# One attention stream and one mixing stream over all eight sequences, and the norm's power by logarithm and exponential

## The chip, the core and the metric

The kernel runs on one core of a Trainium2 chip, in one launch. The core has five engines with queues of their own: TensorE (PE in the profile; PEld is its weight load), VectorE (DVE), ScalarE (ACT), GpSimd (POOL) and SyncE (SP, which here only issues DMAs). The metric is the device time of one execution in microseconds; the time given is the median of the executions shown.

## What is computed

The reference is two transformer layers over 8 sequences of 256 tokens with 256 channels, all in float32:

```python
x = x + attention(layernorm(x))      # w = x W^T; q, k, v are w, RMS-normed per head (16 heads of 16)
                                     # score = softmax over j + softmax over i; y = (score v) W
x = x + experts_0(layernorm(x))      # 4 experts, 2 per token: silu(x w1) * (x w3) @ w2, weighted
                                     # by the router, plus a shared expert on every token
x = x + time_mixing(layernorm(x))    # RWKV: k, v, r of shifted tokens; a recurrence over time;
                                     # layer norm; times sigmoid(r); output matrix
x = x + experts_1(layernorm(x))      # 8 experts, 2 per token, gated, with biases
```

The RMS norm needs, for each token and head, (mean of 16 squares + eps) to the power -1/2.

## The kernel before, in words

Tokens stay in SBUF as eight tiles `xs[b]` of 128 partitions by 2 by 256. The sequences are split in two groups, 0 to 4 and 5 to 7 (`GROUPS`), and each expert layer has one object per group: `one` and `two` in layer 0, `three` and `four` in layer 1 (class `Experts`).

**Experts.** For each sequence `norm` (layer norm on DVE with a small power on POOL), `flip` (transpose on PE, copy on ACT) and `judge` (router matmuls) fill the group's logits. `choose` turns them into slots by some forty small DVE operations and two matmuls, so that every expert's tokens lie together, in tiles of 128 rows. `sends` writes each token's normed row to its two slots in DRAM, by indirect DMAs that POOL issues (20 for the large group, 12 for the small). `tiles` is a software pipeline over the tiles (23 and 15 in layer 0, 27 and 19 in layer 1): fetch the rows, transpose, up-projection, activation, transpose, down-projection, a copy `yg` out of PSUM (L839), and a write to DRAM (L840). `combine` gathers each token's two results by indirect DMAs on POOL and adds them to `xs` on DVE (L868); the gathers wait until all tiles of the group are written. `shared` is the shared expert of layer 0, or the bias term of layer 1.

**Attention** (`attention_bounded`). `steps` lays the parts of each sequence out over numbered steps, four steps from one sequence to the next: `norm`, `project_in` (L436, then the RMS norm in L441 to L447), two steps later `turn` (transposes of the normed n, L456), then scores and exponentials (L480, L485, L493), `values` (L511), `to_tokens`, `turn_back`, `project_heads` (L551, L554), and after that the group's `norm`, `flip`, `judge`. PE's order in this stage is the order of the program (`manual_schedule`); the other engines' orders, and PE's elsewhere, come from a planner that goes by the program's order as priority and by modelled times. Each engine then works through its queue in that fixed order.

**Mixing** (`time_mixing`). `rwkv(b)` yields eight times; a sequence starts when the one before has done four of its steps, so two are in flight. Two multiplications (L949, L952) and the small powers of its norms are on POOL, most of the rest on DVE.

**Order.** `weave` interleaves streams in proportion to the numbers given. Before the change the program runs: attention of group 0; `one.choose`; sends and shared of `one` with the first six steps of group 1's attention; 12 tiles of `one` with the rest of that attention; `two.choose`; sends of `two` with the other tiles of `one`; combine of `one`, shared of `two`; mixing of group 0 with the tiles of `two`; `three.choose`; combine of `two`; the weights of layer 1; sends and shared of `three` with six steps of group 1's mixing; tiles of `three` with the rest of it; `four.choose`; sends and shared of `four` with the last tiles of `three`; combine of `three` with the tiles of `four`; combine of `four`, after which the outputs leave.

Of the kernel before, what the change touches and what calls it, by code (L numbers as in the profile page):

```python
# [9 lines left out]
F32 = mybir.dt.float32  # L10
# [57 lines left out]
def two_layers(  # L68
# [57 lines left out]
    minus_half = filled("minus_half", -0.5, (P, TT * NH))  # L126
# [9 lines left out]
    awt = load(const, attn_wt, [P, NC, D], "(c p) o -> p c o", nc.scalar, p=P, name="awt")  # L136
    gv = const.tile([P, 3, DH], F32, tag="gv", name="gv")
    nc.scalar.dma_start(out=gv, in_=g123.partition_broadcast(P))
    aw = load(const, attn_w, [P, NC, D], "(c p) o -> p c o", nc.scalar, p=P, name="aw")
# [265 lines left out]
    def attention_bounded(ap1, ap2, ep, fresh):  # L405
# [21 lines left out]
        def norm(b):  # L427
            seq[b] = dict(xT=turned(layer_norm(ap2, b, "xn"), ap2, "xnT", fresh()[0], nc.scalar))

        def project_in(b):  # L430
# [10 lines left out]
            nc.scalar.activation(sq, pw4, AF.Square)  # L441
            rr = ap2.tile([P, TT, NH], F32, tag="rr", name="rr")
            nc.vector.tensor_reduce(rr, sq, AX.X, ALU.add)
            nc.vector.tensor_scalar(rr, rr, 1.0 / DH, RMS_EPS, ALU.mult, ALU.add)  # L444
            nc.gpsimd.tensor_tensor(rr, rr, minus_half.rearrange("p (t h) -> p t h", h=NH), ALU.pow)  # L445
# [76 lines left out]
        def to_tokens(b, u):  # L522

            q = seq[b]
            if u == 0:
                q["y"] = ap2.tile([P, TT, NH, DH], F32, tag="y", name="y")
# [15 lines left out]
        def turn_back(b):  # L542
            y = seq[b]["y"].rearrange("p t h d -> p t (h d)")
            seq[b]["yT2"] = turned(y, ap2, "yT2", fresh()[0], nc.scalar)
# [11 lines left out]
        def steps(seqs, after):  # L556
# [11 lines left out]
            for i, b in enumerate(seqs):  # L568
# [12 lines left out]
                for k, f in enumerate(after):  # L581
                    at(n + 7 + k, f, b)
            order = (norm, turn, exponentials, project_in, to_tokens, values, turn_back, project_heads) + tuple(after)
            for n in range(max(late) + 1):
                for f, args in sorted(late.get(n, []), key=lambda x: order.index(x[0])):
                    f(*args)
                yield
# [24 lines left out]
    class Experts:  # L612
# [7 lines left out]
        def __init__(self, layer, k, weights, lnp, mp, rt, ps, mm):  # L620
# [7 lines left out]
            self.last = self.seqs == GROUPS[-1]  # L628

        def norm(self, b):  # L630
            if not self.xns:
                self.logit = self.rt.tile([P, self.nt, self.n_experts], F32, tag="logit", name="logit", bufs=2)
            self.xns[b] = layer_norm(self.lnp, b, "xm", bufs=max(len(g) for g in GROUPS))
# [19 lines left out]
        def choose(self):  # L653
# [22 lines left out]
            self.route()  # L676

# [111 lines left out]
        def tiles(self):  # L789
# [46 lines left out]
            def down(j):  # L836
                py = times(hTs.pop(j), self.weights[1], experts.pop(j), n_hidden, D)
                yg = mp.tile([P, D], F32, tag="yg", name="yg", bufs=3)
                nc.vector.tensor_copy(yg, py)  # L839
# [36 lines left out]
    def time_mixing(rp, rp1, wkv_w, ps, pk):  # L876
# [20 lines left out]
        def rwkv(b):  # L897
# [36 lines left out]
            ex, e1 = new("ex", 3), new("e1")  # L934
# [124 lines left out]
    def layers(is_bounded):  # L1059
# [4 lines left out]
        with ExitStack() as pctx, ExitStack() as ctx0, ExitStack() as actx:  # L1064
# [14 lines left out]
            one, two = (Experts(0, k, w0, lnp, mp, rt, ps, mm) for k in range(2))  # L1079
            with ExitStack() as p1:  # L1080
                psum.update(pool=p1.enter_context(tc.tile_pool(name="p1", bufs=1, space=PSUM)), ps=4, sc=4)
                if is_bounded:
# [3 lines left out]
                    steps = attention_bounded(ap1, ap2, ep, lambda: (ps, sc))  # L1086
                    with tc.manual_schedule(engines={ENG.PE}):
                        for _ in steps(GROUPS[0], (one.norm, one.flip, one.judge)):
                            pass
                else:  # L1090
                    for b in GROUPS[0]:
                        one.norm(b), one.flip(b), one.judge(b)
            with ExitStack() as p2:
                psum.update(pool=p2.enter_context(tc.tile_pool(name="p2", bufs=1, space=PSUM)), mm=2, ps=3, sc=3)
                one.choose()
                tiles = one.tiles()
                if is_bounded:
                    attention = steps(GROUPS[1], (two.norm, two.flip, two.judge))
                    with tc.manual_schedule(engines={ENG.PE}):
                        weave((one.sends(), 10), (take(attention, 6), 6), (one.shared(), 5))  # L1100
                        weave((take(tiles, 12), 12), (attention, 13))
                    actx.close()
                else:
                    weave((one.sends(), 10), (one.shared(), 5))
                    weave((take(tiles, 12), 12))
                    for b in GROUPS[1]:
                        two.norm(b), two.flip(b), two.judge(b)
# [3 lines left out]
            two.choose()  # L1111
            weave((two.sends(), 6), (tiles, 13))
# [7 lines left out]
            mixing = time_mixing(rp, rw, wkv_w, ps, sc)  # L1120
            three, four = (Experts(1, k, None, lnp, None, rt, ps, mm) for k in range(2))

            def norm_of(experts):
                def f(b):
                    experts.norm(b), experts.flip(b), experts.judge(b)

                return f

            tiles = two.tiles()
            weave((one.combine(), 5), (two.shared(), 3), (take(tiles, 2), 2))  # L1130
            weave((mixing(GROUPS[0], norm_of(three)), 36), (tiles, 15))
            three.choose()
            weave((two.combine(), 3))
# [7 lines left out]
            ahead = mixing(GROUPS[1], norm_of(four))  # L1141
            weave((three.sends(), 10), (three.shared(), 5), (take(ahead, 6), 6))
            tiles = three.tiles()
            weave((take(tiles, 17), 17), (ahead, 16))
            four.choose()
            weave((take(tiles, 3), 3))
            weave((four.sends(), 6), (four.shared(), 3), (tiles, 9))
# [83 lines left out]
```

## Time and profile before

| | us |
|---|---|
| median of three executions (979.26 to 980.01) | 979.57 |
| the profiled execution | 982.58 |
| its span, first to last instruction | 980.8 |
| PE busy / PEld busy | 748.6 / 460.7 |
| DVE busy | 501.1 |
| ACT busy | 356.0 |
| POOL busy | 261.7 |

The span is the time from the first to the last profiled instruction. Busy time is an engine's own working time; what an engine idles is not by itself lost, since another may set the end. The granted clock tells how much of TensorE's full rate it was given. A row of the timeline gives start and duration in microseconds, engine, line, operation, what is written and read, and in brackets how long the engine had idled and what released it.

### The profile page before, as it was taken

How to read it: one execution, taken by the hardware profiler on the slowest of the kernel's cores; microseconds unless marked ns; L12 is line 12 of the kernel's file. 1: busy time of each engine (PE TensorE's matmuls, PEld its weight loads, DVE VectorE, ACT ScalarE, POOL GpSimd, SP SyncE). 2: the span in 40 equal slices, each digit the busy share in tenths (PEclk: the TensorE clock that was granted, in tenths of full speed). 3: DMA queues.
4: the chain of work that ended last, by engine and by line, in shares of the span. 5: the costliest groups of instructions: out<-in, count | busy, mean ns of one | idle time of the engine just before them, and what ended most of it. 6: DMA issues, size and time to landing. Idle time of an engine off the chain costs nothing. (4 is left out here: it accounts for less than half of the span.)

```text
span 980.8 us, 11031 instructions
## 1 busy us (share of the span) xinstructions
PE 748.6 (76%) x3248; PEld 460.7 (47%) x3248; DVE 501.1 (51%) x1208; ACT 356.0 (36%) x693; POOL 261.7 (27%) x338
## 2 busy tenths in 40 slices
PE   2588885668899997998798869923777876897890
PEld 1234444553445464666565646612444544453450
DVE  4476774224234324113578567766557684335442
ACT  1376651135566722221154345300225252232230
POOL 4423201830200001304412112052723131516104
PEclk9998895897889997999799779965678798799995
DMA  8910000210000002212210000015811111315313
GB/s 275 315 58 1 1 1 6 80 44 11 16 17 22 28 27 76 97 44 89 62 33 17 27 12 11 17 53 168 289 59 44 43 38 33 108 65 165 115 61 105
DMA packets 57762, 66.97 MB, mean 68 GB/s; under 512 B 7480, under 2 KB 51552, under 8 KB 57696
## 3 DMA queue, kind: packets, MB, share of 16 engines
q1 hardware_dynamic: 50016, 48.79, 15.4%
q0 software_dynamic: 6144, 16.79, 5.4%
q10 hardware_dynamic: 1536, 0.60, 0.2%
q8 instruction: 31, 0.51, 0.2%
q14 instruction: 35, 0.29, 0.1%
HBM read 38.61 MB, written 27.54 MB: 67 GB/s over the span
## 5 line engine op out<-in xcount | busy, mean ns | idle before, releaser
L812 PE MATMUL mm<-v1s,xgT 128*128 x184 | 97.8, 654 | 0.8 <-ACT xgT L806 0.7
L865 POOL DMA_INDIRECT y<-back,slot x64 | 62.1, 970 | 126.4 <-DMA back<-yg 94.0
L806 ACT COPY hT<-ps 128x256 f32<-128x256 f32 (+1 forms) x84 | 39.3, 467 | 131.5 <-PE ps L804 131.5
L736 POOL DMA_INDIRECT sent<-xm,slot x64 | 63.8, 997 | 71.7 <-DVE pick L711 53.9
L812 PE MATMUL mm<-w1s,xgT 128*128 x152 | 78.9, 642 | 1.1 <-issue 0.3
L812 PE MATMUL mm<-w3s,xgT 128*128 x152 | 73.1, 603 | 3.3 <-DVE h L834 3.3
L480 PE MATMUL sc<-qT,kT 32*128 32x512 f32 x256 | 62.9, 741 | 15.0 <-ACT e L493 13.1
L177 POOL TENSOR_TENSOR rs<-mv,eps_ln 128x2 f32<-128x2 f32 x32 | 7.6, 238 | 248.8 <-DVE mv L175 226.8
L494 DVE TENSOR_REDUCE s<-e 128x2 f32<-128x512 f32 x96 | 60.2, 678 | 25.6 <-ACT e L493 25.3
L493 ACT ACTIVATE e<-sc,minus 128x512 f32<-128x512 f32 x96 | 59.2, 694 | 37.1 <-PE sc L480 37.1
L812 PE MATMUL mm<-w2s,hT 128*128 x304 | 72.5, 380 | 0.0
L834 DVE TENSOR_TENSOR h<-h,mm 128x512 f32<-128x512 f32 x38 | 25.9, 681 | 76.5 <-PE mm L812 65.8
L445 POOL TENSOR_TENSOR rr<-rr,minus_half 128x32 f32<-128x32 f32 x8 | 43.5, 5437 | 76.2 <-DVE rr L444 76.2
L804 PEld LDWEIGHTS ps<-ident,h 128*128 128x128 f32 x244 | 31.7, 147 | 66.8 <-issue 34.1
L804 PE MATMUL ps<-ident,h 128*128 128x128 f32 x244 | 44.1, 289 | 23.0 <-DVE h L828 11.1
L839 DVE COPY yg<-mm 128x256 f32<-128x256 f32 x84 | 35.3, 420 | 50.3 <-PE mm L812 50.1
L825 DVE TENSOR_TENSOR hb<-mm,b1rows 128x512 f32<-128x512 f32 x46 | 31.6, 688 | 53.2 <-PE mm L812 47.8
L806 ACT COPY xgT<-ps 128x256 f32<-128x256 f32 x84 | 30.9, 370 | 74.1 <-PE ps L804 73.6
L812 PEld LDWEIGHTS mm<-w2s,hT 128*128 128x128 f32 x304 | 54.8, 190 | 5.9
L812 PE MATMUL mm<-v2s,hT 128*128 x184 | 49.2, 390 | 1.4 <-ACT hT L806 0.8
L868 DVE SCALAR_TENSOR_TENSOR x<-y,share,x 128x256 f32<-128x256 f32 x64 | 30.7, 484 | 38.1 <-DMA y<-back,slot 38.0
L812 PEld LDWEIGHTS mm<-w3s,xgT 128*128 128x128 f32 x152 | 29.2, 195 | 42.4 <-issue 34.2
(208 smaller groups left out, 1396.0 us busy)
## 6 DMA issues: line engine op xcount, KB each, us to landing
xg<-sent SPq DMA_DIRECT2D x84, 128.0 KB, 2.0
back<-yg SPq DMA_DIRECT2D x84, 128.0 KB, 1.7
sent<-zero SPq DMA_DIRECT2D x46, 128.0 KB, 1.9
x<-in_x_dram SPq DMA_DIRECT2D x8, 256.0 KB, 3.9
w1s<-in_w_dram SPq DMA_DIRECT2D x4, 512.0 KB, 9.6
w3s<-in_w_dram SPq DMA_DIRECT2D x4, 512.0 KB, 9.2
w2s<-in_w_dram SPq DMA_DIRECT2D x4, 512.0 KB, 10.4
v1s<-in_v1g_dram SPq DMA_DIRECT2D x8, 256.0 KB, 5.9
```

The lines of the kernel that those rows point to most:

```text
L445: nc.gpsimd.tensor_tensor(rr, rr, minus_half.rearrange("p (t h) -> p t h", h=NH), ALU.pow)
L480: nc.tensor.matmul(pa, lhsT=q["kT"][rows, u, ts(t, P)], rhs=q["qT"][rows, u], start=True, stop=True)
L493: nc.scalar.activation(e, pa, AF.Exp, bias=minus)
L494: nc.vector.tensor_reduce(q["s"][:, t, h : h + 2], e, AX.X, ALU.add)
L736: inst = nc.gpsimd.indirect_dma_start(out=self.sent, out_offset=self.index(k, t), in_=self.xns[self.seqs[t // TT]][:, t % TT, :], in_offse ...
L804: nc.tensor.transpose(pt[:, c, :], src[:, ts(c, P)], ident)
L806: nc.scalar.copy(to, pt)
L812: nc.tensor.matmul(po.unsqueeze(1), lhsT=lhsT[:, c, :], rhs=w[:, ds(e, 1), c, :], start=(c == 0), stop=(c == n - 1))
L825: nc.vector.tensor_tensor(hb.unsqueeze(1), ph.unsqueeze(1), self.weights[2][:, ds(e_dve, 1), :], ALU.add)
L839: nc.vector.tensor_copy(yg, py)
L865: nc.gpsimd.indirect_dma_start(out=y, out_offset=None, in_=self.back, in_offset=self.index(k, at))
L868: nc.vector.scalar_tensor_tensor(xs[b][:, t, :], y, self.share[:, k, at : at + 1], xs[b][:, t, :], ALU.mult, ALU.add)
```

## The change

- The power of the RMS norm leaves POOL. The mean of squares plus eps stays in `ms`; ACT takes its logarithm and the exponential of -1/2 of that, and three DVE operations make one Newton step on the result.
- Attention is one stream over all eight sequences. The choice of `one` is a step of that stream, as soon as its last sequence is judged; from there its sends and shared experts are woven into the stream, with `ps` as their PSUM banks. The choice of `two` is a step of the stream as well. All tiles of `one` follow it, with sends and shared of `two`.
- Mixing is one stream over all eight sequences, cut into pieces: 18 steps with the tiles of `two`, three with its combine, then the weights of layer 1, steps until `three` is chosen, 12 with sends and shared of `three`, the rest with 8 of its tiles. The norms and routers of `three` and `four`, and their choices, are called as sequences end (`take_in`).
- `xm` has eight buffers instead of five; `xn`, `xnT`, `y`, `yT2` and `ex` have one instead of two.
- In layer 0 the copy `yg` is ACT's instead of DVE's. The load of `gv` is issued before that of `awt`.

```diff
@@ project_in
+            ms = ap2.tile([P, TT, NH], F32, tag="ms", name="ms")
+            nc.vector.tensor_reduce(ms, sq, AX.X, ALU.add)
+            nc.vector.tensor_scalar(ms, ms, 1.0 / DH, RMS_EPS, ALU.mult, ALU.add)
             rr = ap2.tile([P, TT, NH], F32, tag="rr", name="rr")
-            nc.vector.tensor_reduce(rr, sq, AX.X, ALU.add)
-            nc.vector.tensor_scalar(rr, rr, 1.0 / DH, RMS_EPS, ALU.mult, ALU.add)
-            nc.gpsimd.tensor_tensor(rr, rr, minus_half.rearrange("p (t h) -> p t h", h=NH), ALU.pow)
+            nc.scalar.activation(rr, ms, AF.Ln)
+            nc.scalar.activation(rr, rr, AF.Exp, scale=-0.5)
+            r3 = ap2.tile([P, TT, NH], F32, tag="r3", name="r3")
+            nc.vector.tensor_tensor(r3, rr, rr, ALU.mult)
+            nc.vector.scalar_tensor_tensor(r3, r3, -0.5, ms, ALU.mult, ALU.mult)
+            nc.vector.scalar_tensor_tensor(rr, r3, 1.5, rr, ALU.add, ALU.mult)
@@ steps
-                for k, f in enumerate(after):
-                    at(n + 7 + k, f, b)
+                m = after[b]
+                at(n + 7, m.norm, b)
+                at(n + 8, m.flip, b)
+                at(n + 9, m.judge, b)
+                if b == m.seqs[-1]:
+                    at(n + 9, m.choose)
@@ Experts
+        def take_in(self, b):
+            self.norm(b), self.flip(b), self.judge(b)
+            if b == self.seqs[-1]:
+                self.choose()
...
-            self.xns[b] = layer_norm(self.lnp, b, "xm", bufs=max(len(g) for g in GROUPS))
+            self.xns[b] = layer_norm(self.lnp, b, "xm", bufs=B)
...
-                nc.vector.tensor_copy(yg, py)
+                if self.layer:
+                    nc.vector.tensor_copy(yg, py)
+                else:
+                    nc.scalar.copy(yg, py)
@@ rwkv
-            ex, e1 = new("ex", 3), new("e1")
+            ex, e1 = new("ex", 3, bufs=1), new("e1")
@@ layers, bounded path
+                    one.mm = ps
                     with tc.manual_schedule(engines={ENG.PE}):
-                        for _ in steps(GROUPS[0], (one.norm, one.flip, one.judge)):
-                            pass
...
-                psum.update(pool=p2..., mm=2, ps=3, sc=3)
-                one.choose()
...
-                    attention = steps(GROUPS[1], (two.norm, two.flip, two.judge))
-                        weave((one.sends(), 10), (take(attention, 6), 6), (one.shared(), 5))
-                        weave((take(tiles, 12), 12), (attention, 13))
+                        attention = steps(range(B), group_of)
+                        while not one.chosen:
+                            next(attention)
+                        weave((one.sends(), 10), (attention, 12), (one.shared(), 5))
+                    one.mm = mm
...
-            two.choose()
-            weave((two.sends(), 6), (tiles, 13))
+            weave((two.sends(), 6), (one.tiles(), 25), (two.shared(), 3))
...
-            weave((one.combine(), 5), (two.shared(), 3), (take(tiles, 2), 2))
-            weave((mixing(GROUPS[0], norm_of(three)), 36), (tiles, 15))
-            three.choose()
-            weave((two.combine(), 3))
+            weave((one.combine(), 5), (take(tiles, 2), 2))
+            weave((take(mixing, 18), 18), (tiles, 15))
+            weave((take(mixing, 3), 3), (two.combine(), 3))
...
-            ahead = mixing(GROUPS[1], norm_of(four))
-            weave((three.sends(), 10), (three.shared(), 5), (take(ahead, 6), 6))
+            while not three.chosen:
+                next(mixing)
+            weave((three.sends(), 10), (three.shared(), 5), (take(mixing, 12), 12))
             tiles = three.tiles()
-            weave((take(tiles, 17), 17), (ahead, 16))
-            four.choose()
-            weave((take(tiles, 3), 3))
-            weave((four.sends(), 6), (four.shared(), 3), (tiles, 9))
+            weave((take(tiles, 8), 8), (mixing, 12))
+            weave((four.sends(), 6), (four.shared(), 3), (tiles, 21))
             weave((three.combine(), 5), (four.tiles(), 21))
```

## The prediction

> **What bounds the kernel now.** I read the page first: TensorE is busy 76% of the span, at a clock granted below full.
>
> ```profile
> span 980.8 us, 11031 instructions
> PE 748.6 (76%) x3248; PEld 460.7 (47%) x3248; DVE 501.1 (51%) x1208; ACT 356.0 (36%) x693; POOL 261.7 (27%) x338
> PE   2588885668899997998798869923777876897890
> PEclk9998895897889997999799779965678798799995
> ```
>
> So PE sets the time where it is full, and holes and slow clock are what can be won. Then the table of stretches, cut where the stages change (columns: stretch, length and busy us of PE, PEld, DVE, ACT, POOL, clock, DMA):
>
> ```profile
> 28.00:160.00 132.00, 101.59 (x708) 54.72 (x708) 82.74 (x211) 71.84 (x173) 32.51 (x30) 0.88 0.18 60
> 160.00:228.00 68.00, 45.95 (x188) 33.80 (x188) 22.66 (x69) 17.20 (x30) 31.92 (x26) 0.81 0.14 47
> 228.00:371.00 143.00, 130.56 (x603) 69.62 (x602) 49.31 (x114) 79.38 (x140) 7.95 (x7) 0.89 0.07 22
> 371.00:452.00 81.00, 76.69 (x290) 49.34 (x290) 21.56 (x82) 21.48 (x39) 12.51 (x14) 0.94 0.22 70
> 484.00:669.00 185.00, 144.49 (x572) 98.42 (x570) 132.74 (x276) 70.84 (x106) 41.10 (x48) 0.88 0.08 26
> 669.00:716.00 47.00, 23.68 (x80) 15.87 (x81) 25.17 (x80) 8.02 (x16) 25.35 (x26) 0.57 0.73 242
> ```
>
> In order: attention of sequences 0-4; choice, sends and shared experts; attention of 5-7 with 12 tiles; 11 tiles; mixing of 0-4; the hole between the mixing groups. Two stretches are poor: 160 to 228, and 669 to 716, where PE works half the time at 0.57 clock. Third, the timeline inside one attention period (start, duration):
>
> ```profile
> 82.87 0.68 DVE L443 TENSOR_REDUCE rr<-sq 128x32 f32<-128x512 f32 x1
> 83.58 0.18 DVE L444 TENSOR_SCALAR rr<-rr 128x32 f32<-128x32 f32 x1
> 83.84 5.43 POOL L445 TENSOR_TENSOR rr<-rr,minus_half 128x32 f32<-128x32 f32 x1 [3.48 <-DVE rr L444]
> 89.30 0.69 DVE L447 TENSOR_TENSOR n<-ps,rr 128x512 f32<-128x512 f32 x1 [5.54 <-POOL rr L445]
> ```
>
> PE has nothing from 85.6 to 90.05 (4.42 us before L456): POOL's power is late, once a period of 23.2 us. Last, the mixing rhythm, from DVE's timeline:
>
> ```profile
> 588.18 0.69 DVE L895 TENSOR_TENSOR dx<-x 128x512 f32<-128x512 f32 x1 [2.68 <-ACT x L900]
> 625.72 0.67 DVE L895 TENSOR_TENSOR dx<-x 128x512 f32<-128x512 f32 x1
> 638.47 0.69 DVE L895 TENSOR_TENSOR x<-x,sc 128x512 f32<-128x512 f32 x1 [1.75 <-PE sc L993]
> 668.84 0.69 DVE L895 TENSOR_TENSOR x<-x,sc 128x512 f32<-128x512 f32 x1 [0.68 <-PE sc L993]
> ```
>
> A sequence begins (dx) 37 us after the one before and ends (x) 50 us after its own begin, 43 us when alone: latency of a chain, two in flight.
>
> **What the Trainium skill says.** "ScalarE: Activation LUTs", Table sets: Ln and Exp lie together in one set, natural_log_exp_and_others; What ACT_TABLE_LOAD costs: 1283 ns and a drain of some 1380. The trace has 1283 ns, and the next activation 11 ns later where its input was there, so I take 1.28 and no drain. "TensorE: Matmul & The Clock Gate", Part 1: after about 3.4 us idle PE runs at half rate for as long. It agrees: clock 0.92 over 66.8 to 85.6, but 1.00 over 70 to 85.6, just after a hole of 4.3 us. "GPSIMD Engine Reference", section 3, has elementwise work about twice as slow as on VectorE; the power is beyond that, 5437 ns where L444 takes 182 for the same shape.
>
> **The change, part by part.**
>
> *Power.* It takes away 8 powers on POOL of 5.43 us and adds two small ACT operations (nearest row, L668: 0.24 each) and three DVE ones (0.19 each, as L444). No trace shows whether Ln and Exp share a loaded set. The first load, at 15.2, serves copy, Square and Exp and has no Ln yet; the general path asks for the joint set by name (L290), this path does not. So I take two loads a sequence (2.57 us of ACT); the other end is none. ACT is in the middle of an exponential when the mean is ready at 83.8: from 84.3, 1.28+0.24+1.28+0.24 to 87.3, DVE 0.7 with hops, n 0.69, so PE turns at 88.75 in place of 90.05. Gain 1.3 a period, and some 0.4 of clock; 3.9 without loads; minus 0.2 if Ln queues behind all exponentials, to 85.8. The loads sit in ACT's hole of 5.4 us before the next copy; were that full they'd cost 2.6. Behind Ln in ACT's queue stand that step's last exponentials, and PE's values wait for those. POOL's queue is freed: at 176.2 a power between two sends held DVE, and so PE, for 8.2 us.
>
> *First turn.* ACT is idle there, the first load hides: n begins 2.8 earlier; gv ahead of awt gives up to 0.5 (one issue of 0.48 on ACT's queue), awt is needed only at 17.1. Turn at 28.7 becomes 25.5.
>
> *One attention stream.* Turns now at 28.7, 46.3, 66.8, 90.1, 113.3. After: 25.5, +15.9, +18.8, +5 x 21.5 = 167.7 for sequence 7. From turn to judged: 46.1, as 113.3 to 159.4. The choice (9.2 us, 159.4 to 168.6) hides under the matmuls of sequences 5-7, as do the sends (20 x 1.27); uncovered they cost those 9.2 and 25. On POOL the sends stand before the norms of 6 and 7, on DVE the choice before reductions of exponentials, which have slack until PE's values one step later. Five shared steps go in: 1.89+1.89+1.99 of matmul and some 2.5 of waiting for Silu, its load, and the product, as PE's order is fixed: 41.4, less 6.9 of holes in that tail (1.2, 2.3, 3.4) = 34.5. They hold three of four ps banks. End 248.3.
>
> *Tiles of one, alone.* Between 387.8 and 445.6 eleven tiles come out 5.78 apart, PE full, clock 1. 23 x 5.78 = 132.9, 8 to begin (1.4 tile steps until the row is full, an estimate), three shared of two 17.3 (3 x 5.77); sends of two lie under it. Silu and Exp no longer alternate: 19 loads (24 us of ACT) in 228 to 371 go. Last tile 406.5, now 449.5. The output copy moves to ACT (0.37 for 0.42), off a DVE that mixing needs.
>
> *Begin of mixing.* 20 gathers stand in POOL's queue before the norm's small power: 34 us from 449.5 to dx at 483.5, kept: 440.5.
>
> *One mixing stream.* Fifteen tiles (87 us of PE) now fall on 18 steps rather than 40: two intervals at 40. Then five with few tiles: DVE adds up to some 25 us a sequence (reciprocal 3.3, mixes 21.3/8 = 2.7, scans 40.4/8 = 5.0, eleven operations of 128x512 at 0.69, z, statistics and two norms 6.9), so not under 25, and not over today's 37; 31, the middle, taken. 440.5+80+155+50 = 725.5, now 824.7. Weights (680 to 706 today), the choice of three, its sends and two's gathers (12) lie under it, and would cost their own 26, 9, 27 and 15 where nothing covered them; in POOL's queue they stand before mixing's products (at 712 k came after the sends). On SP the 26 weight loads still stand before three's fetches, now well ahead of them. One ex buffer: the next sequence fills it four steps later, when it is read out; taken as nothing, 3 us each if the steps slip. xn, y and yT2 with one buffer likewise: refilled four steps on. Xm has eight, so no send holds a norm.
>
> *End.* Choice of four 8.8: 734. Ten tiles of three done by then (8 are woven in); 36 left at 3.02 (their spacing from 916 to 948) 108.7, shared 6.3 (3 x 2.1, rows L764 and L768 by eight), holes 11.1 as at 891 to 916, then 25.7 from last tile to end as now: 885.8.
>
> Sum: 980.8 becomes 885.8: 43 less until the last tile of one, 56 less in mixing, 4 more after. The profiled execution took 982.58, 1.8 over its span and 3.0 over the median: 887.6, or 884.6 as a median. I take 885.
>
> **Rivals.**
> - Ln and Exp in one set: 2.6 less at each of eight turns: 864. For it: the skill; against: no preload here. 13%.
> - Mixing keeps its rhythm: seven intervals of 37 are 24 more, and sends behind it leave four tiles done, not ten, 18 more: 927. For it: 185 us for five sequences with DVE only 72% busy. 25%.
> - Slower: mixing is a chain that POOL holds. Gathers that wait for two's last tile, and then 20 sends, stand before its norms and products; the interval from 709.5 to 774.9 is 65 us already. Seven intervals of 50 are 115 more: 1000. From a mean of 47 it is slower than before. Against: only that one interval is over 41. 10%.
> - No effect (the holes merely move): nothing in the sum cancels so exactly; 1%.
>
> The above forecast has 51%.
>
> **How the numbers follow.** Its own range is 865 to 912 (attention period 20 to 23.5, mixing interval 28 to 34). For 8 in 10 take in the joint set and the slow mixing: 845 to 950. Faster by over 0.2%, about what such a measurement can tell: 89%; within: 1%; slower: 10%.
>
> **What would show it.** Turns of L456 about 21.5 apart with two loads at each Ln; POOL without 5.4 us operations; choice of one before the attention's end, no PE hole at it; tile outputs of one 5.8 apart at clock 1, the last near 407; dx rows about 31 apart from the third, and the last x near 726; PE poor, clock near a half, between two's last tile and three's first. Wrong if mixing's intervals stay over 40, if PE stalls at the shared steps for more than 5 us each, or if three's tiles begin only after mixing.

## The result and the profile after

The changed kernel takes 972.13 us (median of four, 971.55 to 973.21) where the kernel before takes 979.69 (979.26 to 980.01): a ratio of 0.9924, 95% interval 0.9907 to 0.9942. It is faster by 0.8%; the forecast was 885, and neither its own range (865 to 912) nor the wide one (845 to 950) holds the result. The profiled execution took 971.55 with a span of 969.7, 11.1 us shorter than the span before. In all the runs one execution (3834.26 us, of the run with the later choice) was in a slow state, and it is left out of the times below.

The page of the changed kernel, span and busy times, then PE's busy tenths and its granted clock in 40 slices:

```profile
span 969.7 us, 11030 instructions
...
PE 737.1 (76%) x3248; PEld 462.9 (48%) x3248; DVE 492.4 (51%) x1194; ACT 355.0 (37%) x735; POOL 217.4 (22%) x330
...
PE   2689987748879999996999846553558759997890
...
PEclk9898898878879999998999957665577978998895
```

POOL lost its powers (261.7 to 217.4 busy), PE's share stayed at 76%. The poor stretch of attention is still there (7, 7, 4 in slices 7 to 9; a slice is 24.2 us). The other one, two slices before (2, 3), is now seven slices wide: 4, 6, 5, 5, 3, 5, 5 from slice 24 on (from 558 us), with a clock of 5 to 7 tenths. The table of stretches, cut where the stages change (columns as before: stretch, length and busy us of PE, PEld, DVE, ACT, POOL, clock, DMA):

```profile
28.00:160.00 132.00, 115.49 (x848) 61.20 (x851) 102.36 (x268) 106.09 (x239) 12.38 (x30) 0.88 0.19 63
160.00:210.00 50.00, 26.99 (x169) 16.78 (x170) 24.77 (x87) 21.85 (x44) 21.10 (x24) 0.73 0.19 64
...
273.00:427.00 154.00, 153.19 (x582) 98.26 (x582) 21.39 (x40) 46.17 (x97) 11.59 (x12) 0.98 0.16 49
445.00:557.00 112.00, 103.03 (x414) 68.48 (x412) 66.49 (x131) 48.25 (x84) 21.13 (x25) 0.98 0.12 37
557.00:730.00 173.00, 88.31 (x284) 61.92 (x285) 125.27 (x274) 31.74 (x57) 60.02 (x68) 0.61 0.24 77
730.00:786.00 56.00, 39.75 (x142) 26.48 (x142) 35.88 (x77) 18.90 (x34) 12.28 (x16) 0.80 0.08 24
786.00:944.00 158.00, 141.70 (x514) 84.30 (x513) 65.80 (x151) 47.95 (x126) 46.07 (x53) 0.92 0.32 100
```

In order: attention of sequences 0 to 4; the choice of one and its sends; tiles of one, alone; mixing with the tiles of two; mixing without tiles; its end, with the first tiles of three; the rest of the experts. PE is full with tiles of one, and nearly full (103 of 112) as long as there are tiles of two. Then for 173 us it works 88, at a clock of 0.61. That stretch is where the answer lies.

Three marks divide each span: the first `dx` of mixing, the routing matmul of four's choice, the end. The count in the fourth column is of the 46 tiles of layer 1 whose output was made before four's choice. All are from profiled executions:

| kernel | to first dx | mixing, to four's choice | after it | tiles of layer 1 done | span |
|---|---|---|---|---|---|
| before | 483.5 | 350.8 | 146.5 | 16 | 980.8 |
| changed | 445.4 | 340.2 | 184.1 | 4 | 969.7 |

So 38.1 us were won before mixing, 10.6 in it, and 37.6 lost after it. The twelve tiles not yet made, at the 3.02 us of their spacing, are 36.2 of those 37.6. Mixing and all that follows took 497.3 before and takes 524.3: the mixing part of the change loses 27.

### The profile page after: what moved, and what is told of

Read it like the earlier page. It is cut to its first block, busy times and chain, and to the rows that moved or that the text cites. A ratio compares the mean times of both kernels' runs of the same rounds, so it can differ in the third digit from the quotient of the medians.

```text
span 969.7 us, 11030 instructions
## 1 busy us (share of the span) xinstructions
PE 737.1 (76%) x3248; PEld 462.9 (48%) x3248; DVE 492.4 (51%) x1194; ACT 355.0 (37%) x735; POOL 217.4 (22%) x330
## 5 line engine op out<-in xcount | busy, mean ns | idle before, releaser
L837 PE MATMUL mm<-v1s,xgT 128*128 x184 | 95.7, 644 | 0.0
L837 PE MATMUL mm<-w1s,xgT 128*128 x152 | 75.0, 615 | 1.0 <-issue 0.3
L943 PE MATMUL sc<-mix,rw 128*128 128x256 f32 x192 | 56.0, 454 | 8.1 <-DVE mix L937 8.0
L829 PE MATMUL ps<-ident,h 128*128 128x128 f32 x244 | 42.1, 280 | 22.1 <-DVE h L853 10.0
L850 DVE TENSOR_TENSOR hb<-mm,b1rows 128x512 f32<-128x512 f32 x46 | 31.7, 689 | 53.2 <-PE mm L837 52.1
L191 PE MATMUL ps<-ident,xm 128*128 128x128 f32 x64 | 14.4, 355 | 51.5 <-DVE xm L181 51.5
L943 PEld LDWEIGHTS sc<-mix,rw 128*128 128x128 f32 x192 | 42.8, 231 | 20.0 <-DVE mix L937 12.8
L487 PE MATMUL sc<-qT,kT 32*128 32x512 f32 x256 | 50.7, 767 | 2.0 <-DVE qT L468 2.0
```

The costliest lines, as they stand in the source:

```text
L487: nc.tensor.matmul(pa, lhsT=q["kT"][rows, u, ts(t, P)], rhs=q["qT"][rows, u], start=True, stop=True)
L829: nc.tensor.transpose(pt[:, c, :], src[:, ts(c, P)], ident)
L837: nc.tensor.matmul(po.unsqueeze(1), lhsT=lhsT[:, c, :], rhs=w[:, ds(e, 1), c, :], start=(c == 0), stop=(c == n - 1))
L850: nc.vector.tensor_tensor(hb.unsqueeze(1), ph.unsqueeze(1), self.weights[2][:, ds(e_dve, 1), :], ALU.add)
L943: nc.tensor.matmul(po[:, o, :], lhsT=w[:, c, ts(o, P)], rhs=mix[:, c, :], start=(c == 0), stop=(c == NC - 1))
```

## The experiments

The runs were made on several chips. The kernel before takes 978 to 980 us on some and 998 to 1004 on others, so each ratio is to the kernel before on the same chip (it can lie 0.4% from the quotient of the two medians, within its interval), and the three stretches are read beside it.

### Each part alone

The attention part alone: the changed kernel with mixing, from its pool to the end, as it was before (`ex` kept at one buffer).

```diff
-            mixing = time_mixing(...)(range(B), lambda b: group_of[b].take_in(b))
...
-            weave((take(mixing, 18), 18), (tiles, 15))
...
+            weave((mixing(GROUPS[0], norm_of(three)), 36), (tiles, 15))
+            three.choose()
...
+            ahead = mixing(GROUPS[1], norm_of(four))
+            weave((three.sends(), 10), (three.shared(), 5), (take(ahead, 6), 6))
...
+            weave((take(tiles, 17), 17), (ahead, 16))
+            four.choose()
...
```

> The attention part of the change alone (one attention stream, choice of one and its sends inside it, shared of two beside tiles of one, power by Ln and Exp), with the mixing of the kernel before (two groups). Theory 'mixing gave it back': the mixing block of before needs 497.3 us from its first dx to the end (483.5 to 980.8); begun at 445.4, as in the changed kernel, it ends near 943, a time of about 945 us, faster than the whole change. Rival 'the mixing stream earned its part': 972 or more. Between 955 and 965 both took a share.

The mixing part alone: the kernel before with that block of the changed kernel.

> The mixing part of the change alone, with the attention of the kernel before (its four small buffers single, to make room for eight xm). Theory 'mixing gave it back': the changed mixing needs 524.3 us from its first dx to the end (445.4 to 969.7); begun at 483.5 it ends near 1008, about 1010 us, slower than before by 3%. Rival 'the loss comes from what the attention part pushes into mixing': 980 or less.

Measured, with 95% intervals: attention alone 959.14, ratio 0.9606 (0.9569 to 0.9642); mixing alone 1015.82, ratio 1.0185 (1.0143 to 1.0227). Their stretches are 454.0, 355.9, 149.7 and 486.8, 341.7, 183.9. Each stretch goes with its own part of the code: mixing alone has the changed kernel's 341 and 184, attention alone the short end of before, with 16 tiles done against 4. The mixing stream loses time whatever stands ahead of it, and the single `ex` buffer, which attention alone has too, is not what lengthens the end. By its time attention alone misses the 945 of its theory and falls between 955 and 965: of the 16.9 us that its span is over the theory's, 8.6 are there at the first dx (454.0 for 445.4) and 8.3 come after it (505.6 for 497.3), on a chip where the kernel before is 20 us slower too. The changed kernel itself was then run on another chip on which the kernel before takes 998:

> The changed kernel itself, unedited, beside the others on one chip, because the kernel before took 1000.9 us on the chip of the last four runs. If that chip slows all kernels alike, its ratio to the kernel before is 0.992 as at first; if it slows single stages, the ratio differs and the stage is to be named by the marks (turns, choice, first dx, judged, last tile).

It took 978.04, ratio 0.9826 (0.9778 to 0.9875), with stretches 449.3, 340.6, 184.7; so the whole change is worse than its attention part alone, whose interval lies below. A pair on one chip, meant to tell why the kernel before differs so between chips, met one of the quick ones:

> The kernel before itself, unedited, with a profile on the chip drawn here. On a chip where it takes about 1000 us, some 20 us more than in its first profile must show in its marks: theory 'its mixing is the slower part' has the first dx within 4 us of 483.5 and first dx to end near 512 (497.3 at first); rival 'its attention is' has the first dx near 500. On a chip where it takes 979 the marks are those of the first profile.

> The changed kernel, unedited, on the same chip as the kernel before: first dx at 445 to 450 and first dx to end 524 to 526, as in its two other profiles. Mixing's loss is the difference of the two stretches on this one chip: 27 us by the first profiles, 14 if the kernel before is slower in mixing here.

They took 977.71, ratio 1.0002 (0.9988 to 1.0016), and 970.23, ratio 0.9908 (0.9892 to 0.9924), with stretches 478.6, 351.2, 145.7 and 447.3, 340.1, 180.2: on one chip 31.3 won ahead of mixing, 23.4 lost from there. In which stage the kernel before is slower on the other chips stays open, for it has no profile there. The profiles of the other runs do show a difference. On the chips where the kernel before takes 998 to 1004, every kernel with the attention stream of the change has DVE idle for 12 to 17 us during the sends of `one`, and ACT beside it, with nothing in the profile that releases DVE; on the chips where it takes 978 to 980 there is no such wait. In the changed kernel's profile from the chip of 998:

```profile
207.71 0.69 DVE L561 TENSOR_TENSOR x<-x,ps 128x512 f32<-128x512 f32 x1 [16.36 <-remote]
```

"remote" means that no instruction in the profile is seen to release it; the matmuls that it reads from had ended at 191.2, and the last send was issued at 203.9. What holds the two engines is not known, and attention is best compared between chips of one kind.

### Where mixing lost it

One edit spreads the tiles of two as before; one, with two's tiles left dense, weaves three's tiles in earlier; a third run has both.

```diff
-            weave((take(mixing, 18), 18), (tiles, 15))
+            weave((take(mixing, 36), 36), (tiles, 15))            # spread
...
-            weave((three.sends(), 10), (three.shared(), 5), (take(mixing, 12), 12))
+            weave((three.sends(), 10), (three.shared(), 5), (take(mixing, 6), 6))      # early
-            weave((take(tiles, 8), 8), (mixing, 12))
-            weave((four.sends(), 6), (four.shared(), 3), (tiles, 21))
+            weave((take(tiles, 17), 17), (mixing, 14))
+            weave((four.sends(), 6), (four.shared(), 3), (tiles, 12))
```

> The changed kernel with one edit: the fifteen tiles of two are spread over 36 steps of mixing, as before, in place of 18. Theory 'the dense weave slows the first sequences and leaves PE empty afterwards': from the first dx to the judging of sequence 4 falls from 223 us towards the 193 of before, and about 25 us of that arrive at the end: 947. Rival 'the tiles only move, and mixing's latency sets the time': within 5 us of 972. Third, if only the missing tiles of three matter: the end stays at 972 though sequence 4 is judged earlier.

> The changed kernel with two's tiles dense as they are (over 18 steps), but three's sends over 6 steps and 17 of its tiles over the last 14 steps. Theory 'the two losses are separate': 8 to 10 us less than the changed kernel, as the pair (21.6) less the spread alone (12 to 13) says. Rival 'the tiles of three pay only once sequence 4 is judged earlier': under 3 us.

> Two edits in mixing: tiles of two over 36 steps, as in the run with that edit alone, and three's sends over 6 steps in place of 12 with 17 of its tiles over the last 14 steps in place of 8 over 8. Theory 'what the tiles of three lost is the rest of the loss': some 20 of them are done when sequence 7 is judged (4 in the changed kernel), mixing's last three sequences take 10 to 15 us longer, and the end comes 10 to 15 us earlier than with the spread alone, to a ratio near 0.955. Rival 'they slow mixing by as much as they save': within 4 us of the spread alone (ratio 0.967).

| kernel | us | ratio (95%) | to first dx | mixing | after it | tiles done |
|---|---|---|---|---|---|---|
| changed, chip of early3 | 978.04 | 0.9826 (0.9778 to 0.9875) | 449.3 | 340.6 | 184.7 | 4 |
| spread | 965.27 | 0.9669 (0.9633 to 0.9705) | 454.1 | 326.0 | 185.3 | 4 |
| early alone | 964.93 | 0.9635 (0.9588 to 0.9683) | 452.3 | 357.4 | 153.8 | 15 |
| both | 956.45 | 0.9600 (0.9558 to 0.9642) | 448.8 | 350.9 | 153.8 | 15 |

The table of stretches of the spread, from the first dx to the end of two's tiles, then to three's first tiles, then to four's choice (columns as above):

```profile
454.00:565.00 111.00, 90.22 (x338) 60.27 (x337) 78.69 (x151) 44.54 (x74) 25.76 (x29) 0.91 0.10 31
565.00:728.00 163.00, 95.97 (x361) 67.59 (x360) 111.20 (x259) 42.95 (x72) 56.65 (x64) 0.71 0.27 86
728.00:780.00 52.00, 37.39 (x140) 24.74 (x139) 32.85 (x73) 16.15 (x32) 11.48 (x16) 0.83 0.09 26
```

The same of early alone:

```profile
452.00:564.00 112.00, 103.06 (x414) 68.67 (x412) 66.49 (x131) 48.53 (x85) 21.11 (x25) 0.98 0.12 37
564.00:740.00 176.00, 96.07 (x305) 65.18 (x306) 124.86 (x273) 34.89 (x65) 60.92 (x70) 0.61 0.24 79
740.00:810.00 70.00, 60.30 (x253) 39.23 (x251) 47.87 (x100) 30.10 (x62) 18.14 (x25) 0.96 0.17 54
```

The spread takes PE work out of its full stretch (103 to 90) and puts it into the empty one, whose clock rises from 0.61 to 0.71: mixing is 14.6 shorter, the end stays. Early alone leaves both stretches nearly as they were and fills the third (60.30 of 70, clock 0.96): mixing is 16.8 longer, the end 30.9 shorter. From first dx to the end the changed kernel takes 520 to 525 (three profiles), either edit 511, both 504.7: 9 to 14 each, 16 to 21 together, so they partly pay for the same empty PE time; the rival for early alone (under 3 us) falls. The ratios agree: 1.6% and 1.9% alone, 2.3% together, with intervals of half a per cent; the step from early alone to both is by itself within them. The expectations were met in part only. With the spread, three's choice comes 215.2 us after the first dx in place of 226.8, where the kernel before has 196.8, and 965 is not 947; both together have 15 tiles done, not 20, and mixing is 25 us longer than with the spread alone, not 10 to 15.

### Choice, sends and tables in attention

The timeline of the changed kernel at the choice of one, in its first profile:

```profile
162.53 1.05 PE L668 MATMUL ps<-gw,xmT 128*128 128x4 f32 x8
...
168.21 0.16 DVE L675 COPY logit<-ps 128x8 f32<-128x8 f32 x1
...
172.40 0.23 DVE L707 TENSOR_TENSOR took<-hot,hot 128x40 f32<-128x40 f32 x1
...
172.68 0.65 PE L713 MATMUL ps<-took,before_w 128*128 128x40 f32 x2 [9.09 <-DVE took L707]
...
202.98 0.96 POOL L761 DMA_INDIRECT sent<-xm,slot  x1 [0.30 <-issue]
203.96 0.21 POOL L177 TENSOR_TENSOR rs<-mv,eps_ln 128x2 f32<-128x2 f32 x1
...
205.00 0.74 DVE L181 TENSOR_SCALAR xm<-x,mv,rs 128x256 f32<-128x256 f32 x2 [12.18 <-POOL rs L178]
```

The logits are ready at 163.6, but DVE copies them only at 168.2, behind the attention's own work, and ends the choice at 172.4. L713 stands in PE's fixed order ahead of everything of the next step, so PE waits 9.09 us for it. The twentieth send is issued at 203.0, and only behind it comes the norm of sequence 5: DVE's `xm` waits 12.18 for it, and PE 13.07 (13.12 in the profile of the pair, on a chip of the same kind). Three edits, each a run: the choice two steps later; the table set named once; the latter with the norms of attention on ACT.

```diff
-                    at(n + 9, m.choose)
+                    at(n + 11, m.choose)                                               # later
...
+                    nc.scalar.preload_act_table_set("natural_log_exp_and_others")      # preload
                     steps = attention_bounded(ap1, ap2, ep, lambda: (ps, sc))
```

> One edit: the choice of one is issued two steps of attention later, so that TensorE's fixed order has more matmuls between the last logits of one and the matmul of its choice. Theory 'PE's order turns the chain of choice into a hole': the hole of 9.1 us at 164 to 173 goes, and the last tile of one and the end come 5 to 9 us earlier than in the changed kernel; the sends begin some 6 us later, and the hole behind them on POOL stays. Rival 'the hole only moves on, to the sends': no more than 2 us.

> One edit: the set of tables with Ln and Exp is loaded once by name ahead of the attention, so that the 16 loads of 1.28 us there go (the prediction's first rival, which priced them at 2.6 us at each of eight turns, 21 us). Theory 'the loads are on the path of the turn': the hole ahead of each turn falls from 1.9 to nothing, and the end comes 10 to 20 us earlier than in the changed kernel. Rival 'PE stays behind for another reason (its fixed order, the choice)': under 4 us.

> Two edits within attention: the set with Ln and Exp is loaded once by name, and the norms take their root by Ln and Exp on ACT, as the power does, in place of POOL. Theory 'the sends on POOL hold the norms': the hole of 13.1 us at 192 to 205 goes to under 3, the 16 loads of 1.28 go, turns come some 20 us apart in place of 21.5, and the last tile of one and the end come 15 to 25 us earlier than in the changed kernel. Rival 'PE is full there anyway': under 5 us.

The later choice: 962.57 (three executions, 960.89 to 968.89), ratio 0.9680 (0.9608 to 0.9751), beside 978.04 for the changed kernel on its chip; the profiled span is 13.9 shorter, 12.7 of it ahead of the first dx (436.6 against 449.3). On this chip the changed kernel's own holes are 9.11 us at the choice and 6.88 ahead of the norm of sequence 5. Both go, not one:

```profile
175.98 0.23 DVE L707 TENSOR_TENSOR took<-hot,hot 128x40 f32<-128x40 f32 x1
...
176.72 0.31 PE L713 MATMUL ps<-took,before_w 128*128 128x40 f32 x2
...
180.17 0.19 POOL L177 TENSOR_TENSOR rs<-mv,eps_ln 128x2 f32<-128x2 f32 x1 [13.39 <-DVE n_e L721]
...
181.73 0.78 PE L191 MATMUL ps<-ident,xm 128*128 128x128 f32 x4 [2.18 <-DVE xm L181]
...
185.72 1.20 POOL L761 DMA_INDIRECT sent<-xm,slot  x1 [4.58 <-DVE pick L736]
```

PE does not wait for L713 at all, and since the sends begin at 185.7, the norm of sequence 5 (180.2) is ahead of them on POOL; PE waits 2.18 for it. So 13.8 us of holes go, and 12.7 arrive at the first dx. On this chip, though, the norm of the changed kernel had waited for the idle DVE shown above, not for POOL's queue: that the sends alone hold it is seen on the quick chips, and there no run has the later choice by itself.

The preload: 949.34, ratio 0.9686 (0.9642 to 0.9731), on a chip where the kernel before takes 979.33. It is the largest single gain, 21 to 24 us of span (967.6 and 969.7, in the two profiles from such chips, to 946.2); the last turn comes at 154.7 in place of 173.6, the first dx at 424.9 in place of 445.4. The timeline of one turn in the changed kernel:

```profile
75.20 1.28 ACT L447 ACT_TABLE_LOAD   x1
...
76.77 0.23 ACT L447 ACTIVATE rr<-ms 128x32 f32<-128x32 f32 x1 [0.29 <-DVE ms L444]
...
77.49 1.28 ACT L448 ACT_TABLE_LOAD   x1
...
78.79 0.23 ACT L448 ACTIVATE rr<-rr 128x32 f32<-128x32 f32 x1
...
80.55 1.12 PE L463 MATMUL ps<-ident,n 128*128 128x128 f32 x4 [1.94 <-DVE n L454]
```

The same turn with the preload:

```profile
67.98 0.23 ACT L447 ACTIVATE rr<-ms 128x32 f32<-128x32 f32 x1 [1.88 <-DVE ms L444]
...
68.58 0.23 ACT L448 ACTIVATE rr<-rr 128x32 f32<-128x32 f32 x1
...
70.34 0.66 PE L463 MATMUL ps<-ident,n 128*128 128x128 f32 x4 [0.55 <-DVE n L454]
```

From the logarithm to the turn (L447 to L463, start to start) 3.78 becomes 2.36, PE's hole 1.94 becomes 0.55, and the four transposes take 0.66 in place of 1.12, at a granted clock of 1.00 in place of 0.50. The exponentials of the scores, next in ACT's queue, no longer wait for two loads either; what that adds was not measured by itself.

The norms on ACT: 965.92, ratio 0.9685 (0.9642 to 0.9729), 10.7 of span less than the changed kernel on its chip. That is half the gain of the preload, which it contains, but the preload ran on a quick chip, and the two are not told apart from the chip. Its timeline at sequence 5:

```profile
185.75 0.96 POOL L773 DMA_INDIRECT sent<-xm,slot  x1 [0.31 <-issue]
...
189.77 0.69 DVE L573 TENSOR_TENSOR x<-x,ps 128x512 f32<-128x512 f32 x1 [16.37 <-remote]
...
191.10 1.28 ACT L182 ACT_TABLE_LOAD   x1
...
192.62 1.28 ACT L183 ACT_TABLE_LOAD   x1
...
195.98 1.23 PE L203 MATMUL ps<-ident,xm 128*128 128x128 f32 x4 [5.70 <-DVE xm L193]
```

The norm no longer needs POOL, but DVE has stood idle until after the last send, so the sends are not tested here. What the run does show: once the shared experts' Silu has come in (its load is at 163.2), the named set is gone, and each later norm pays two loads again (from 191.1, 226.0 and 249.0). This one has its row 4.05 us after the statistics, where POOL's power gives 1.1. The expected "under 3 us" for that hole failed: 5.70.

The power back on POOL was the test of the prediction's first step.

```diff
-            nc.scalar.activation(rr, ms, AF.Ln)
-            nc.scalar.activation(rr, rr, AF.Exp, scale=-0.5)
...
+            nc.gpsimd.tensor_tensor(rr, rr, minus_half.rearrange("p (t h) -> p t h", h=NH), ALU.pow)
```

> The changed kernel with the power back on POOL. Theory (the prediction's term): the hole ahead of each turn grows from about 1.9 to 4.4 us, 8 periods give 15 to 20 us more, and the first turn comes 3 later: 985 to 990. Rival 'the holes of choice and sends hide it': under 976.

It took 994.83, ratio 0.9948 (0.9929 to 0.9967), on a slower chip than the 985 to 990 was reckoned for. The holes ahead of the turns are 4.3 to 4.4 us again, the first dx comes at 467.9, 18.6 to 22.5 later than in the three profiles of the changed kernel (18.6 on the chip of its kind), and mixing and the end are the same (340.9, 184.4). The rival falls.

### A norm that needs no POOL

To free the norms from POOL's queue in mixing too, all roots of 128x2 went to DVE.

```diff
-        nc.gpsimd.tensor_tensor(rs, mv[:, :, 1], eps_ln.to_broadcast([P, TT]), ALU.add)
-        nc.gpsimd.tensor_tensor(rs, rs, minus_half[:, 0:TT], ALU.pow)
...
+        nc.vector.tensor_scalar(ve, var, eps, None, ALU.add)
...
+        nc.vector.tensor_scalar(half_bits, ve.bitcast(I32), 1, None, ALU.logical_shift_right)
+        nc.vector.tensor_scalar(rs.bitcast(I32), half_bits, -1.0, float(0x5F3759DF), ALU.mult, ALU.add)
...
+        for _ in range(3):
+            nc.vector.tensor_tensor(r4, rs, rs, ALU.mult)
+            nc.vector.scalar_tensor_tensor(r4, r4, -0.5, ve, ALU.mult, ALU.mult)
+            nc.vector.scalar_tensor_tensor(rs, r4, 1.5, rs, ALU.add, ALU.mult)
```

> One edit: every norm's root of 128x2 is made on DVE (a first guess from the bits and three Newton steps, 12 small instructions) in place of two instructions on POOL, in attention and in mixing. Theory 'sends and gathers on POOL hold the norms': the hole of 7 to 13 us at 192 to 211, part of the wait for the first xr (5.7), and the holes of 9.1 and 7.4 us in sequence 5's mixing go: 15 to 25 us less than the changed kernel. Against it, the 12 instructions may take 1 us longer in a chain that mixing runs three times a sequence: in the stretch where POOL is free the interval of 31 grows by up to 3. Rival 'the holes are made by what stands ahead on DVE too': under 5 us in all.

It is slower than before: 1000.69, ratio 1.0215 (1.0184 to 1.0245). From the statistics to the first normed row it takes 3.90 us in attention, where POOL's two instructions take 1.1. In mixing it is worse: at the last norm of a sequence (`z`) the median of the eight is 8.0 us in place of 1.3, because other work of DVE comes between the twelve links (one of them runs from 708.6 to 717.4). The stretches are 457.7, 360.4, 180.7. The gain failed, and so did the bound on the cost (1 us a norm): the longer chain comes at every norm, POOL's queue at a few.

### All together

> All that helped, together: choice two steps later, roots of the norms on DVE, the joint set loaded once, two's tiles over 36 steps, three's sends over 6 steps and 17 of its tiles over 14. If the savings add (14 for the choice, 15 for the norms, 8 for the loads, 21 for the tiles, less what is counted twice), the time is near 930, a ratio of 0.93. Rival 'they overlap, since PE's work fills what is left': about 945, a ratio of 0.947.

This one held the roots on DVE, and took 962.01, ratio 0.9837 (0.9803 to 0.9871), worse than theory and rival: mixing went to 379 us. Without them:

> The edits that each helped, without the roots on DVE: the joint set loaded once, choice two steps later, two's tiles over 36 steps, three's sends over 6 steps and 17 of its tiles over 14. Theory 'separate losses that add': 23 for the loads, 14 for the choice, 21 for the tiles, 58 less than the changed kernel, a ratio to the kernel before near 0.933. Rival 'one loss seen several times, PE's own work fills the rest': 35 less, near 0.957.

And with the gathers of one woven into mixing:

```diff
-            weave((one.combine(), 5), (take(tiles, 2), 2))
-            weave((take(mixing, 36), 36), (tiles, 15))
+            gathers = one.combine()
+            weave((take(gathers, 1), 1), (take(tiles, 2), 2))
+            weave((take(mixing, 36), 36), (tiles, 15), (gathers, 18))
```

> As the combination without roots on DVE, and one's gathers woven into the first steps of mixing in place of ahead of them, so that some five of them stand behind the first norm on POOL. Theory 'the gathers on POOL set the begin of mixing': the first dx comes 5 to 7 us sooner after the last tile of one (19 us now), and 4 to 6 us of it reach the end. Rival 'the first sequence then waits at its next use of POOL': under 2 us.

Measured on one chip, where the kernel before takes 1003.83: 926.30, ratio 0.9245 (0.9198 to 0.9293), and 921.32, ratio 0.9202 (0.9158 to 0.9247). The rival's 35 falls; that the gains add in full is not shown as surely. From the 0.9826 of a like chip to 0.9245 is 5.8% of 1000 us, the 58 expected (the 0.933 was reckoned from 0.992), with intervals of half a per cent; in times it is 52 us (from 978.04), in spans 49.5 (from 974.6), and the changed kernel was not run on this chip. Stretches are 420.1, 351.2, 153.8 and 415.1, 348.8, 153.1. In the first, the first dx comes 29.2 us sooner than in the changed kernel on the like chip, where loads and choice alone gave 20.4 and 12.7; from there to the end it is 20.3 shorter, where both edits in mixing gave 20.6. From the last tile of one to the first dx it takes 16.9 us in place of 19.0 with the gathers woven: less than the 5 to 7 expected; 3 of the 5 us are already there ahead of the last tile, in a stage that the edit does not touch, so that the gathers' own share is 2 and the rest is not told apart from noise. Page of the last kernel:

```profile
span 917.0 us, 11010 instructions
...
PE 717.0 (78%) x3248; PEld 448.1 (49%) x3248; DVE 487.3 (53%) x1194; ACT 342.8 (37%) x727; POOL 219.4 (24%) x330
...
PE   2898998867889999978979798253569795896980
...
PEclk9999999768999999998899899575578996997995
```

It beats both kernels. What is left is the notch of slices 26 to 30, between two's last tile (571.8) and three's first (695.0).

## Why the prediction was wrong

The end was put at a span of 885.8 and came at 969.7, 83.9 later. By the prediction's own steps:

| step | predicted | measured | difference |
|---|---|---|---|
| last tile of one | 406.5 | 426.5 | +20.0 |
| from there to the first dx | 34 | 18.9 | -15.1 |
| two intervals of mixing with two's tiles | 80 | 94.4 | +14.4 |
| five intervals with few tiles | 155 | 187.7 | +32.7 |
| last sequence, dx to x | 50 | 48.2 | -1.8 |
| last x to the end | 160.3 | 194.0 | +33.7 |

The step that failed is the mixing stream with the end that follows from it: 80.8 us in three rows. Of these the edits in mixing win back 16 to 21; what the rest is made of is read from the timelines and was not tried. The 20.0 of attention are for the most part made up by the begin of mixing.

**Power: right.** Two loads a sequence, no drain beyond the 1.28, turns 21.5 apart: the turns came at 25.0, 40.8, 59.8, 80.5, 101.9, 124.3, 144.9. Of what the Trainium skill states in "ScalarE: Activation LUTs", the joint set of the section Table sets is there, but where that section counts one load for a logarithm and an exponential, the trace has two until the set is named (the preload); and the drain of the section What ACT_TABLE_LOAD costs is not in the trace: Exp begins 0.02 us after its load. The rival "joint set", priced at 2.6 us at each of eight turns (21), measures 21 to 24.

**The choice "hides": wrong.** The step said that 9.2 us would lie under the matmuls of sequences 5 to 7. PE's order is written by hand in this stage, and what stands behind a waiting matmul can't hide it: 9.09 us of hole. It was named for the shared steps ("as PE's order is fixed") and not applied to the choice's own two matmuls.

**The sends: wrong.** The prediction put them before the norms on POOL and priced that at nothing here: 13.07 us at sequence 5. Both holes together are 22.2 in the first profile, about the 20 us of the first row. The run with the later choice bears out such a sum on its own chip: 13.8 us of holes less, 12.7 at the first dx.

**Tiles of one: right**, 5.8 apart. **Begin of mixing: wrong, in the forecast's favour.** It put the 34 us down to twenty gathers on POOL. In the kernel before only ten of them stand ahead of the first norm's power, and the normed row is ready at 467.2; PE turns it 15 us later, behind the shared experts of `two`:

```profile
466.76 0.41 DVE L181 TENSOR_SCALAR xr<-x,mv,rs 128x256 f32<-128x256 f32 x1
...
482.25 0.60 PE L191 MATMUL ps<-ident,xr 128*128 128x128 f32 x4
```

The change moves these beside the tiles of `one`, and the forecast did not count that: 18.9 us are left. The parts alone agree: 18.8 with the attention part, which moves them, 34.4 with the mixing part, which leaves them. Without this the miss would be 99 us.

**Mixing: the rhythm "31" was met, its reach wrong.** The rows of `dx` of sequences 2 to 7 in the timeline of DVE, a `z` that waits for POOL, and the last `x`:

```profile
539.79 0.69 DVE L923 TENSOR_TENSOR dx<-x 128x512 f32<-128x512 f32 x1 [2.46 <-ACT x L928]
...
579.62 0.69 DVE L923 TENSOR_TENSOR dx<-x 128x512 f32<-128x512 f32 x1
...
610.47 0.69 DVE L923 TENSOR_TENSOR dx<-x 128x512 f32<-128x512 f32 x1 [0.29 <-ACT x L928]
...
638.35 0.63 DVE L923 TENSOR_TENSOR dx<-x 128x512 f32<-128x512 f32 x1
...
684.59 0.68 DVE L923 TENSOR_TENSOR dx<-x 128x512 f32<-128x512 f32 x1
...
699.65 0.99 DVE L1007 TENSOR_SCALAR z<-ps,mv,rs 128x256 f32<-128x256 f32 x2 [11.39 <-POOL rs L1004]
...
727.53 0.69 DVE L923 TENSOR_TENSOR dx<-x 128x512 f32<-128x512 f32 x1 [0.37 <-ACT x L928]
...
775.70 0.69 DVE L923 TENSOR_TENSOR x<-x,sc 128x512 f32<-128x512 f32 x1 [2.09 <-PE sc L1021]
```

Between 579.62 and 638.35 the intervals are 30.9 and 27.9; as 31 was only the middle of 25 and 37, that it fits is in part luck. Ahead of them the tiles of two fill PE (41.2, 53.2 and part of 39.8): the forecast gave them two intervals, 80 us, though fifteen tiles are 87 us of PE by its own figure, and they ended 112 us after the first dx. After them come the choice of three, weights and twenty sends on POOL (46.2, 42.9), behind which `z` waits 11.39. All seven average 40.3. That is the rival "mixing keeps its rhythm" (37, "four tiles done, not ten"): four tiles were done, and this rival was given 25% and 927 us. The slower rival's threshold, a mean of 47, was not reached.

**The end: wrong with it.** The step took ten tiles of three as done and 36 left. The list of its own ends names the case: "if three's tiles begin only after mixing". Three's first output is at 755.0, 20 us before the last x. Six tiles at 3.02 are 18 of the 33.7; the rest is wider holes between the tiles (the spacing exceeds 3.02 by some 31 us in all between 792 and 911, where 17.4 were allowed for shared experts and holes), argued from the marks and not tried by itself.

The error behind the last two rows is one of kind: the forecast summed the shortening of mixing's chain and kept PE's work out of it. What PE doesn't do beside the chain it does after it. From first dx to four's choice PE worked 260.0 us of 347 before (147.50 and 112.46 busy, 484 to 831), and 231.1 of 341 after (103.03, 88.31 and 39.75): 29 us of work moved behind mixing, for a mixing stretch only 10.6 us shorter.

## What to carry to other kernels

When two long streams of work are rearranged around a chain of latency, add up the work of the bounding engine that still lies beside the chain, not only the chain: work that is packed densely early leaves a hole later, and what then has to follow is paid in full. A step "hidden" in a stage with a hand-written order needs a look at what stands behind it in that order and on each queue that it passes, POOL's sends among them. And where two functions can share a table set, name the set, and mind which later function throws it out.

## What was not expected of the hardware

A hole costs more than its length: after the 13.07 us of idling eight matmuls of 128x256 took 3.57 us, at a granted clock of 0.50, and the next eight 1.89, at 1.00.

```profile
206.49 3.57 PE L800 MATMUL ps<-xmT,sw1s 128*128 128x256 f32 x8
209.90 1.89 PE L800 MATMUL ps<-xmT,sw3s 128*128 128x256 f32 x8
```

The 128x2 power that POOL does in 0.70 us is hard to beat: twelve dependent DVE instructions of about 0.15 us each took 2.8 us longer from statistics to row in attention, and 6.7 us longer at `z`, where DVE's other work came between. And the same kernel before takes 979 us on one chip and 1004 on another, while the changed one moves from 972 to 978: a ratio of 0.992 on one chip was 0.983 on the next.
